# Node scores by GpSimd products and VectorE sums, and denominators summed inside layer 0, in a four-layer graph network kernel

## The chip, the cores and the metric

The kernel runs on one core of a Trainium2 chip. A core has five engines that each work through their own instructions in order and wait for one another through semaphores: TensorE (PE, matrix products into PSUM; its weight loads are listed as PEld), VectorE (DVE), ScalarE (ACT), GpSimd (POOL) and SyncE (SP, which only issues DMAs here). The metric is the device time of one execution in microseconds, lower is better.

## What is computed

The input is x with 8 batches of 2048 nodes of 64 features, and a 2048 x 2048 adjacency matrix. Four graph layers follow, each as `x = layernorm(x + layer(x))`. Layer 0 is a graph convolution with weights mixed for each node from an embedding of 16 numbers; layer 1 is a hypergraph attention; layers 2 and 3 are plain graph convolutions. The change touches the end of layer 0's loop, where the first steps of layer 1 are done already for the rows that are finished:

```python
h = x @ W
s = jax.nn.leaky_relu(h @ a_node, 0.2)
logits = jnp.where(maskEN[None, :, :] > 0, s[:, None, :], NEG)
alpha = jax.nn.softmax(logits, axis=-1)
agg = jnp.einsum('ben,bnf->bef', alpha, h)
beta = jax.nn.sigmoid((h @ a_gn)[:, None, :] + (agg @ a_ge)[:, :, None])
...
industry = jnp.einsum('nm,bmf->bnf', adj / deg, x @ W_ind)
```

So each node needs, for each of the 8 batches, two scores: `h @ a_node`, whose exp becomes its softmax weight, and `h @ a_gn`. The softmax is done without dividing first: `aggp` sums exp(s) h over the nodes of each hyperedge, `denp` sums exp(s), and `agg` is their quotient.

## The kernel before

The nodes are cut into 16 rows of 128 (NT = 16), and a row's tile is 128 nodes x 512 numbers (8 batches x 64 features, B = 8, C = 64). float32 products run as two passes on TensorE, which is why the profile counts 8 for 4 of them.

**Layer 0** (`layer0`) is one loop over j from 0 to 16. Turn j does the 8 weighings of row j (`weigh`, g = 0 to 7): 24 matmuls each (L1035) into one of two PSUM tiles, and four VectorE instructions (L1046) that read this tile and add it to the row's residue r. Between the weighings stand the other steps, some of row j, some of the row behind (j - 1, j - 2) and some of the rows ahead (j + 1, j + 2). All of it stands in `program_order`, which ties the instructions of each engine into exactly the order in which they are written. Nothing can overtake on its engine. In a turn:

- after weighing 0, 1 and 2: the three steps of the norm of row j - 1 (`normed`: sum, centring and square; sum of squares and root; reciprocal and the two products that give x1). After weighing 1 also `scaled` (GpSimd: the mask of the next row times its scale, `ms`, and the count tree `cs`).
- after weighing 2: `first_terms` of row j + 1: GpSimd adds y_hi and y_lo to y1 (L971), TensorE transposes y1 (`try`, in a helper, L152) and multiplies the bias (`bp`, L979), ScalarE copies both, GpSimd makes the new residue r (L984).
- after weighing 3: the whole y2 product of row j + 1 (L998, 32 matmuls), the transposes of x1 of row j - 1 (`to_features`, `trx`), compares and masks on VectorE.
- after weighing 6: `second_term` (four transposes), `scores` of row j - 1, `gather` of row j - 2.
- after weighing 7: `degrees`, and `project` of row j - 1: 8 products (`hp`, L1113) give h and the industry part; ScalarE copies h (L1129), then the high part of the industry (L1130), VectorE forms the low part (L1131), and GpSimd multiplies h by exp(s) to `hs` (L1138).

`scores` works from the transposed x1: `wa` holds W a_node and W a_gn, computed once in `load_weights`, and four products per row (`sgp`, L1092) give both scores. `gather` (L1143) adds `hs` times the hyperedge memberships `md` into `aggp`.

**Layer 1** (`layer1`) starts with `md` for all rows on GpSimd (L551), 16 products for the denominators (`denp`, L556), their reciprocal `rden`, and `agg`.

The last turn (j = 16) has no weighings: it is a plain chain of norm, transposes, scores, gather, h and gather for row 15.

Of the kernel before, what the change touches and what calls it, by code (L numbers as in the profile page):

```python
# [8 lines left out]
F32 = mybir.dt.float32  # L9
# [9 lines left out]
P = 128  # L19
# [27 lines left out]
def r_(ap):  # L47
    return ap.bitcast(F32R)
# [3 lines left out]
def kernel(  # L52
# [454 lines left out]

    @with_exitstack
    def layer1(
        stack, own, wts, fcw_sb, fcb_sb, av_sb, fcg_sb, vecs, pm, es, hgr, aggp, agg_st, h_sb,  # L510
        i_hi, i_lo, mask_tile, times_mask,
    ):

# [20 lines left out]
        with tc.tile_pool(name="fa", bufs=2) as fa:  # L534
# [10 lines left out]
                for n, k in (("ftr", 1), ("fmm", 1))  # L545
            )
            with program_order():
                md = fa.tile([P, NT, 2, E], F32, tag="md", name="md", bufs=1)
                for q in range(NQ):
                    t = slice(4 * q, 4 * q + 4)  # L550
                    nc.gpsimd.tensor_copy(  # L551
                        md[:, t], pm[:, t].unsqueeze(2).to_broadcast([P, 4, 2, E])
                    )
                denp = ps_tr.tile([P, B], F32, tag="den", name="denp")
                for j in range(NT):
                    nc.tensor.matmul(  # L556
                        denp, md[:, j].rearrange("p h e -> p (h e)"), es[:, j, :],
                        start=j == 0, stop=j == NT - 1,
                    )
                rden = fa.tile([P, B], F32, tag="rden", name="rdene", bufs=1)  # L560
                nc.vector.tensor_scalar(rden, denp, TINY, None, op0=ALU.max)
                nc.vector.reciprocal(rden, rden)
                agg = fa.tile([P, BC], F32, tag="hs", name="agg", bufs=3)
                nc.vector.tensor_tensor(b_view(agg), b_view(aggp), bcast(rden), ALU.mult)

# [329 lines left out]
    def layer0(  # L895
# [3 lines left out]

        h_sb, wb, wa, vecs, av_sb, pm, es, hgr, aggp = layer1s
        raws, msk, terms, resid, norm, srow = {}, {}, {}, {}, {}, {}
        x1s, xTs, hps, hss, mds = {}, {}, {}, {}, {}

# [181 lines left out]
            nc.scalar.copy(xTs[j], tr)  # L1087

        def scores(j):
            sp = ps_tr.tile([P, NP, 2, 2], F32, tag="tr", name=f"sgp_{j}")  # L1090
            for pr in range(NP):
                nc.tensor.matmul(  # L1092
                    sp[:, pr].rearrange("p i h -> p (i h)"), xTs[j][:, pr, :],
                    wa.rearrange("p i h -> p (i h)"), start=True, stop=True,
                )
            sg = tile("sg", f"sg_{j}", (P, NP, 2))
            nc.scalar.copy(sg, sp[:, :, 0, :])
            nc.scalar.copy(hgr[:, j, 0, :].rearrange("p (r h) -> p r h", h=2), sp[:, :, 1, :])
            ej = es[:, j, :]
            nc.vector.scalar_tensor_tensor(  # L1100
                ej.rearrange("p (r h) -> p r h", h=2), sg, 0.2, sg, op0=ALU.mult, op1=ALU.max
            )
            nc.vector.tensor_scalar(ej, ej, TOP, None, op0=ALU.min)
            nc.scalar.activation(ej, ej, AF.Exp)

        def project(j):

            mm = ps_p.tile([P, 2, 2, 4 * C], F32, tag="pp", name=f"hp_{j}")
            mm = mm.rearrange("p h l (m x) -> p h (l m) x", m=2)
            for pr in range(NP):  # L1110
                for h in range(2):
                    rs = slice(h * 64, (h + 1) * 64)
                    nc.tensor.matmul(  # L1113
                        mm[:, h, pr, :], xTs[j][rs, pr, :], wb[rs], start=True, stop=True
                    )
            md = tile("md", f"md_{j}", (P, 2, E))
            nc.gpsimd.tensor_copy(md, pm[:, j, :].unsqueeze(1).to_broadcast([P, 2, E]))
            mds[j] = md.rearrange("p h e -> p (h e)")

            def by_half(t):  # L1120
                return t.rearrange("p (r h c) -> p h r c", h=2, c=C)


            stay = j >= len(kept_i)
            if stay:
                hi, lo = y_hi[:, j, :], y_lo[:, j, :]
            else:
                hi, lo = (tile(k, f"{k}_{j}", bufs=1) for k in ("ihi", "ilo"))
            nc.scalar.copy(by_half(h_sb[:, j, :]), mm[:, :, :, 0:C])  # L1129
            nc.scalar.copy(r_(by_half(hi)), mm[:, :, :, C:2 * C])  # L1130
            nc.vector.tensor_tensor(  # L1131
                r_(by_half(lo)), mm[:, :, :, C:2 * C], by_half(hi), ALU.subtract
            )
            if not stay:
                for t, kept_part in zip((hi, lo), kept_i[j]):
                    nc.sync.dma_start(kept_part, t)
            hss[j] = tile("hs", f"hs_{j}", bufs=1)
            nc.gpsimd.tensor_tensor(  # L1138
                b_view(hss[j]), b_view(h_sb[:, j, :]), bcast(es[:, j, :]), ALU.mult
            )  # L1140

        def gather(j):
            nc.tensor.matmul(aggp, mds[j], hss[j], start=j == 0, stop=j == NT - 1)  # L1143

        box = tile("box", "flagbox", (P, 256), 1)
        flags = lists_flag(
            box, lambda: ps_tr.tile([P, QW], F32, tag="tr", name="flagp"), pm, wb[:, 0:C],
# [14 lines left out]
        with program_order():  # L1162
# [6 lines left out]
            for j in range(NT + 1):  # L1169
                first = j == 0  # L1170
                if not first:
                    when(j + 2, load_adj)
                when(j + 2, load_x)
                for g in range(8):
                    when(j, weigh, g)
                    if g == 0:
                        when(j - 1, normed, 0)
                        if first:
                            compare(0, 0)
                            compare(0, 1)  # L1180
                            load_adj(2)
                    elif g == 1:
                        when(j - 1, normed, 1)
                        if first:
                            degrees(0)
                        when(j + 1, scaled, 0)
                    elif g == 2:
                        when(j - 1, normed, 2)
                        when(j + 1, first_terms)
                    elif g == 3:  # L1190
                        if j + 1 < NT:
                            for _ in product(j + 1):
                                pass
                        when(j - 1, to_features)
                        when(j + 1, compare, 0)
                        when(j + 1, scaled, 1)
                        if j == NT - 2:
                            for t in range(len(kept_i)):
                                for y, kept_part in zip((y_hi, y_lo), kept_i[t]):
                                    nc.sync.dma_start(y[:, t, :], kept_part)  # L1200
                        when(j + 2, mask, 0)
                        when(j + 2, mask, 1)
                    elif g == 5:
                        when(j + 1, compare, 1)
                        if j:
                            next(flags, None)
                    elif g == 6:
                        when(j + 1, second_term)
                        when(j - 1, scores)
                        when(j - 2, gather)  # L1210
                    elif g == 7:
                        when(j + 1, degrees)
                        when(j - 1, project)
            gather(NT - 1)


    def short_program(top):
# [7 lines left out]


        wb = wts.tile([P, 2 * C], F32, tag="wb", name="wb")
        wa = wts.tile([P, 2, 2], F32, tag="wa", name="wa")
        vecs = wts.tile([P, 3, C], F32, tag="vecs", name="vecs")
        pm = wts.tile([P, NT, E], F32, tag="pm", name="pm")  # L1230
        es = wts.tile([P, NT, B], F32, tag="es", name="es")
        hgr = wts.tile([P, NT, 2, B], F32, tag="hgr", name="hgr")
        fcg_sb = wts.tile([P, 1], F32, tag="fcg", name="fcg_sb")

        def load_weights():
# [8 lines left out]
            block_diag(w2_sb[:, 1, :], w2n)  # L1244
            nc.sync.dma_start(bias2_sb, bias2.partition_broadcast(P))
            block_diag(w3_sb, w3t)
            nc.gpsimd.memset(wa, 0.0)
            prod = wts.tile([P, C], F32, tag="prod", name="prod")
            for h in range(2):
                s = slice(h * 64, (h + 1) * 64)  # L1250
                for i in range(2):
                    nc.vector.tensor_tensor(prod[s], wb[s, 0:C], vecs[s, i, :], ALU.mult)
                    nc.vector.tensor_reduce(wa[s, i, h:h + 1], prod[s], AX.X, ALU.add)

        def prepare(ps, pre):
            for h in range(2):
# [27 lines left out]
        with tc.tile_pool(name="l0", bufs=1) as l0, tc.tile_pool(  # L1284
# [14 lines left out]
            with tc.tile_pool(name="l0s", bufs=2) as l0s, tc.tile_pool(  # L1299
# [3 lines left out]
            ) as ps_p:  # L1303
                layer0(
                    own, l0s, rawp, mskp, ps_acc, ps_tr, ps_p, w_sb, emb_sb, bias_sb, bad, deg,
                    y_hi, y_lo, (h_sb, wb, wa, vecs, av_sb, pm, es, hgr, aggp),
                )
                s1, dinv = cols_of["s1"], cols_of["dinv"]
                nc.vector.tensor_tensor(deg, deg, s1, ALU.mult)
# [15 lines left out]


        x2 = layer1(
            own, wts, fcw_sb, fcb_sb, av_sb, fcg_sb, vecs, pm, es, hgr, aggp, agg_st, h_sb, y_hi,
            y_lo, mask_tile, times_mask,
        )  # L1330

# [695 lines left out]
```

## Time and profile before

| | us |
|---|---|
| median of 3 runs | 1388.19 (1386.91 to 1389.96) |
| profiled execution | 1406.12, of which its span 1404.0 |
| start to 154 (first product) | 154.0, TensorE busy 142.3 |
| 204.4 to 695.8 (steady rows of layer 0) | 491.4, TensorE busy 479.6, VectorE 375.0, GpSimd 215.7, ScalarE 96.8 |
| one such row, 485.40 to 520.46 | 35.06, TensorE busy 34.27, VectorE 26.53, GpSimd 16.01, ScalarE 6.92 |
| 723.3 to 748.4 (the last turn, up to the first exp of layer 1) | 25.1, TensorE busy 16.5, granted clock 0.57 |

The busy times are of single engines, which overlap. The span is the time between the first and the last instruction on the chip in the profiled execution; the times of the other runs are without the profiler. In the lines of the timeline each line has its start, its length, the engine, the line of the code, the operation, what is written and read, how many instructions were merged, and in square brackets how long the engine had been idle and what ended that.

### The profile page before, as it was taken

How to read it: one execution, taken by the hardware profiler on the slowest of the kernel's cores; microseconds unless marked ns; L12 is line 12 of the kernel's file. 1: busy time of each engine (PE TensorE's matmuls, PEld its weight loads, DVE VectorE, ACT ScalarE, POOL GpSimd, SP SyncE). 2: the span in 40 equal slices, each digit the busy share in tenths (PEclk: the TensorE clock that was granted, in tenths of full speed). 3: DMA queues.
4: the chain of work that ended last, by engine and by line, in shares of the span. 5: the costliest groups of instructions: out<-in, count | busy, mean ns of one | idle time of the engine just before them, and what ended most of it. 6: DMA issues, size and time to landing. Idle time of an engine off the chain costs nothing.

```text
span 1404.0 us, 19827 instructions
## 1 busy us (share of the span) xinstructions
PE 1323.9 (94%) x7692; PEld 1033.8 (74%) x7692; DVE 931.5 (66%) x1658; ACT 364.1 (26%) x844; POOL 444.2 (32%) x373
## 2 busy tenths in 40 slices
PE   8999889999999999999977799999998799999997
PEld 6777678888888888888855466666666588888885
DVE  4555357787777777777753767678885666665554
ACT  3000101111111111111221345456665321111111
POOL 0000444444444444444201454546663420000000
PEclk9999999999999999999985788899999899999999
DMA  9865323333333333331504121222220213333551
GB/s 307 210 185 171 124 92 101 100 101 100 100 100 100 100 100 100 100 99 53 210 23 151 52 75 38 75 76 76 75 76 1 91 60 120 120 120 136 180 187 70
DMA packets 91047, 153.00 MB, mean 109 GB/s; under 512 B 12097, under 2 KB 55489, under 8 KB 84673
## 3 DMA queue, kind: packets, MB, share of 16 engines
q1 hardware_dynamic: 88642, 147.46, 31.6%
q10 hardware_dynamic: 2304, 4.20, 0.8%
q8 instruction: 63, 1.03, 0.3%
q14 instruction: 38, 0.31, 0.1%
HBM read 115.97 MB, written 35.66 MB: 108 GB/s over the span
## 4 chain that ended last, share of the span: by engine, by line
PE 91%; DVE 4%; issue 2%; ACT 1%; POOL 1%; DMA 1%; SPq 0%; ACTq 0%; DVEq 0%; POOLq 0%
PE pp L1035 23%; PE a L1273 17%; PE ind L1273 9%; PE y2p L998 9%; PE y1p L469 9%; PE fc L813 3%; PE u L1356 2%; PE df L822 2%; PE gp L708 2%; PE trm L152 1%; PE dp L733 1%; PE try L152 1%; PE aggp L1143 1%; PE hp L1113 1%; PE yp L1385 1%
## 5 line engine op out<-in xcount | busy, mean ns | idle before, releaser
L1046 DVE SCALAR_TENSOR_TENSOR r<-pp,emb_sb,r 128x256 f32<-128x256 f32 x512 | 247.3, 483 | 132.1 <-PE pp L1035 117.5
L1035 PE MATMUL pp<-w_sb,xT 64*128 64x256 f32 x1024 | 163.1, 391 | 11.9 <-PE hp L1113 10.3
L1035 PE MATMUL pp<-w_sb,y1T 64*128 64x256 f32 x1024 | 156.3, 377 | 0.0
L1035 PE MATMUL pp<-w_sb,y2T 64*128 64x256 f32 x1024 | 156.3, 377 | 0.0
L1035 PEld LDWEIGHTS pp<-w_sb,xT 64*128 64x128 f32 x1024 | 98.1, 188 | 35.1 <-issue 15.5
L749 POOL TENSOR_TENSOR ez<-ez,coef 128x1024 f32<-128x1024 f32 x32 | 65.0, 2032 | 153.9 <-DVE ez L747 131.4
L469 PE MATMUL y1p<-x_hi,m 128*128 128x512 f32 x256 | 107.0, 418 | 7.1 <-ACT x_hi L417 7.0
L1035 PEld LDWEIGHTS pp<-w_sb,y1T 64*128 64x128 f32 x1024 | 103.8, 188 | 7.7
L1035 PEld LDWEIGHTS pp<-w_sb,y2T 64*128 64x128 f32 x1024 | 103.8, 188 | 7.7
L1273 PE MATMUL ind<-y_hi,mj_l 128*128 128x512 f32 x256 | 107.1, 418 | 0.7 <-DVE dlt L778 0.7
L998 PE MATMUL y2p<-y_hi,msk 128*128 128x512 f32 x256 | 103.8, 406 | 0.0
L1273 PE MATMUL a<-y_hi,mj_l 128*128 128x512 f32 x256 | 102.5, 401 | 0.0
L469 PE MATMUL y1p<-x_lo,m 128*128 128x512 f32 x256 | 102.3, 400 | 0.0
L998 PE MATMUL y2p<-y_lo,msk 128*128 128x512 f32 x256 | 102.0, 399 | 0.0
L1273 PE MATMUL a<-y_lo,mj_l 128*128 128x512 f32 x256 | 101.6, 397 | 0.0
L1273 PE MATMUL ind<-y_lo,mj_l 128*128 128x512 f32 x256 | 101.5, 396 | 0.0
L1273 PE MATMUL a<-v_hi,mj_l 128*128 128x512 f32 x256 | 100.5, 393 | 0.0
L1273 PE MATMUL a<-v_lo,mj_l 128*128 128x512 f32 x256 | 100.1, 392 | 0.0
L1138 POOL TENSOR_TENSOR hs<-h,es 128x512 f32<-128x512 f32 x16 | 16.7, 1042 | 237.6 <-DVE r L1046 195.4
L950 POOL TENSOR_TENSOR ms<-msk,srow 128x1024 f32<-128x1024 f32 x32 | 77.4, 2418 | 6.4 <-DVE ms L963 5.7
L1273 PEld LDWEIGHTS ind<-y_hi,mj_l 128*128 128x128 f32 x256 | 49.0, 192 | 34.2 <-issue 17.7
L971 POOL TENSOR_TENSOR y<-y_hi,y_lo 128x512 f32<-128x512 f32 x16 | 25.7, 1609 | 133.5 <-PE y1p L469 133.5
(262 smaller groups left out, 2499.2 us busy)
## 6 DMA issues: line engine op xcount, KB each, us to landing
mj_l<-mask SPq DMA_DIRECT2D x48, 1024.0 KB, 4.9
raw<-in_at SPq DMA_DIRECT2D x32, 512.0 KB, 4.8
adj<-in_at SPq DMA_DIRECT2D x64, 256.0 KB, 3.4
mask<-msk SPq DMA_DIRECT2D x32, 512.0 KB, 3.1
xraw<-in_xn SPq DMA_DIRECT2D x8, 512.0 KB, 5.6
oh<-oh SPq DMA_DIRECT2D x16, 256.0 KB, 3.8
xT<-in_xt SPq DMA_DIRECT2D x16, 256.0 KB, 3.0
xs<-in_xn SPq DMA_DIRECT2D x16, 256.0 KB, 2.7
```

What stands on the lines that cost most here:

```text
L152: nc.tensor.matmul(dst, src, ident, start=True, stop=True, is_transpose=True)
L469: nc.tensor.matmul(accs[q][jj], r_(m[:, t, jj * P:(jj + 1) * P]), r_(part[:, mt, :]), start=i + h + t == 0 and part is x_hi, stop=i == 3 a ...
L708: nc.tensor.matmul(gp[:, u, :], r_((oh01, oh23)[i][rs, cols]), r_(part[rs]), start=part is agg_hi, stop=part is agg_lo,)
L749: nc.gpsimd.tensor_tensor(by_b(ez), by_b(ez), per_b(coef, 2 * i, 2), ALU.mult)
L813: nc.tensor.matmul(fc[:, h, :], fcw_sb[rs], sT[rs], start=True, stop=True)
L822: nc.tensor.matmul(df[:, b:b + 1], th[:, b % 2, (b // 2) * P:(b // 2 + 1) * P], av_sb, start=True, stop=True,)
L950: nc.gpsimd.tensor_tensor(ms, m, srow[j].unsqueeze(1).to_broadcast([P, 8, P]), ALU.mult)
L998: nc.tensor.matmul(acc, r_(msk[j, mt // 8][:, mt % 8, :]), r_(part[:, mt, :]), start=mt == 0 and part is y_hi, stop=mt == NT - 1 and part ...
L1035: nc.tensor.matmul(pp[:, h, pl, :], terms[j][name][rs, 2 * bq + pl], w_sb[rs, k, dq * 4 * C:(dq + 1) * 4 * C], start=k == 0, stop=k == K - 1,)
L1046: nc.vector.scalar_tensor_tensor(rb, ppv[:, :, dd, :], emb_sb[:, j, d:d + 1], rb, op0=ALU.mult, op1=ALU.add)
L1273: nc.tensor.matmul(acc, r_(a[:, mt, :]), r_(part[:, mt, :]), start=mt == 0 and part is hi, stop=mt == NT - 1 and part is lo,)
L1356: nc.tensor.matmul(mm[:, i], xT[:, 2 * p2 + i, :], w2_sb, start=True, stop=True)
```

## The change

- `scores` no longer uses TensorE. After h is copied, `project` lets GpSimd multiply h by a_node (into `hss[j]`) and by a_gn (into the tile of x1, which is no longer needed then). `scores` sums each over the 64 features with VectorE, makes the exp as before, and then GpSimd forms h times exp(s).
- `scores` moves from after weighing 6 of the next turn to after weighing 1 of the turn after it (row j - 2 instead of j - 1, as it now needs h).
- `project` copies the high part of the industry ahead of h.
- The denominators are summed at the start of the last turn for rows 0 to 14 (`spread` writes all memberships again, into free buffers) and for row 15 after its scores. `layer1` gets `rden`. In the last turn `gather` of row 14 moves there too, ahead of the denominators.
- `wa` and its computation go.

On GpSimd this gives the order, in each turn from 2 to 14: h times a_node, h times a_gn, ms, three of cs, h times exp(s), y1. On VectorE: four reads of weighing 1, variance sum, sum of scores, leaky relu, clamp, sum for a_gn, four reads of weighing 2. On ScalarE: root, change of table, exp.

```diff
         def scores(j):
-            sp = ps_tr.tile([P, NP, 2, 2], F32, tag="tr", name=f"sgp_{j}")
-            for pr in range(NP):
-                nc.tensor.matmul(
-                    sp[:, pr].rearrange("p i h -> p (i h)"), xTs[j][:, pr, :],
-                    wa.rearrange("p i h -> p (i h)"), start=True, stop=True,
-                )
-            sg = tile("sg", f"sg_{j}", (P, NP, 2))
-            nc.scalar.copy(sg, sp[:, :, 0, :])
-            nc.scalar.copy(hgr[:, j, 0, :].rearrange("p (r h) -> p r h", h=2), sp[:, :, 1, :])
             ej = es[:, j, :]
-            nc.vector.scalar_tensor_tensor(
-                ej.rearrange("p (r h) -> p r h", h=2), sg, 0.2, sg, op0=ALU.mult, op1=ALU.max
-            )
+            sg = tile("sg", f"sg_{j}", (P, B))
+            nc.vector.tensor_reduce(sg, b_view(hss[j]), AX.X, ALU.add)
+            nc.vector.scalar_tensor_tensor(ej, sg, 0.2, sg, op0=ALU.mult, op1=ALU.max)
             nc.vector.tensor_scalar(ej, ej, TOP, None, op0=ALU.min)
             nc.scalar.activation(ej, ej, AF.Exp)
+            nc.vector.tensor_reduce(hgr[:, j, 0, :], b_view(x1s[j]), AX.X, ALU.add)
+            nc.gpsimd.tensor_tensor(
+                b_view(hss[j]), b_view(h_sb[:, j, :]), bcast(ej), ALU.mult
+            )
...
         def project(j):
...
+            nc.scalar.copy(r_(by_half(hi)), mm[:, :, :, C:2 * C])
             nc.scalar.copy(by_half(h_sb[:, j, :]), mm[:, :, :, 0:C])
-            nc.scalar.copy(r_(by_half(hi)), mm[:, :, :, C:2 * C])
...
             hss[j] = tile("hs", f"hs_{j}", bufs=1)
-            nc.gpsimd.tensor_tensor(
-                b_view(hss[j]), b_view(h_sb[:, j, :]), bcast(es[:, j, :]), ALU.mult
-            )
+            for i, t in enumerate((hss[j], x1s[j])):
+                nc.gpsimd.tensor_tensor(
+                    b_view(t), b_view(h_sb[:, j, :]),
+                    vecs[:, i, :].unsqueeze(1).to_broadcast([P, B, C]), ALU.mult,
+                )
...
+        def spread():
+            mds.clear()
+            for q, home in enumerate((1, 2, 3, 5)):
+                md = own.tile([P, 4, 2, E], F32, tag=f"b0_{home}", name=f"md4_{q}")
+                nc.gpsimd.tensor_copy(
+                    md, pm[:, 4 * q:4 * q + 4].unsqueeze(2).to_broadcast([P, 4, 2, E])
+                )
+                for t in range(4):
+                    mds[4 * q + t] = md[:, t].rearrange("p h e -> p (h e)")
+
+        def denominators(lo, hi):
+            for j in range(lo, hi):
+                nc.tensor.matmul(
+                    denp[0], mds[j], es[:, j, :], start=j == 0, stop=j == NT - 1
+                )
...
                         when(j + 1, scaled, 0)
+                        when(j - 2, scores)
+                        if j == NT:
+                            denp.append(ps_acc.tile([P, BC], F32, tag="acc", name="denp")[:, 0:B])
+                            gather(NT - 2)
+                            spread()
+                            denominators(0, NT - 1)
                     elif g == 2:
                         when(j - 1, normed, 2)
                         when(j + 1, first_terms)
...
                     elif g == 6:
                         when(j + 1, second_term)
-                        when(j - 1, scores)
-                        when(j - 2, gather)
+                        if j < NT:
+                            when(j - 2, gather)
...
+            scores(NT - 1)
+            denominators(NT - 1, NT)
+            nc.vector.tensor_scalar(rden, denp[0], TINY, None, op0=ALU.max)
+            nc.vector.reciprocal(rden, rden)
             gather(NT - 1)
```

More of the change, by code (lines that the diff above doesn't have):

```diff
@@ L509, in layer1 @@
     def layer1(
-        stack, own, wts, fcw_sb, fcb_sb, av_sb, fcg_sb, vecs, pm, es, hgr, aggp, agg_st, h_sb,
+        stack, own, wts, fcw_sb, fcb_sb, av_sb, fcg_sb, vecs, rden, hgr, aggp, agg_st, h_sb,
         i_hi, i_lo, mask_tile, times_mask,
@@ L547, in layer1 @@
             with program_order():
[L548 to L552, printed above, removed]
-                    )
-                denp = ps_tr.tile([P, B], F32, tag="den", name="denp")
-                for j in range(NT):
-                    nc.tensor.matmul(
-                        denp, md[:, j].rearrange("p h e -> p (h e)"), es[:, j, :],
-                        start=j == 0, stop=j == NT - 1,
-                    )
-                rden = fa.tile([P, B], F32, tag="rden", name="rdene", bufs=1)
-                nc.vector.tensor_scalar(rden, denp, TINY, None, op0=ALU.max)
-                nc.vector.reciprocal(rden, rden)
                 agg = fa.tile([P, BC], F32, tag="hs", name="agg", bufs=3)
@@ L898, in layer0 @@
     ):
-        h_sb, wb, wa, vecs, av_sb, pm, es, hgr, aggp = layer1s
+        h_sb, wb, vecs, av_sb, pm, es, hgr, aggp, rden = layer1s
         raws, msk, terms, resid, norm, srow = {}, {}, {}, {}, {}, {}
@@ L1089, in scores @@
         def scores(j):
-            sp = ps_tr.tile([P, NP, 2, 2], F32, tag="tr", name=f"sgp_{j}")
-            for pr in range(NP):
-                nc.tensor.matmul(
-                    sp[:, pr].rearrange("p i h -> p (i h)"), xTs[j][:, pr, :],
-                    wa.rearrange("p i h -> p (i h)"), start=True, stop=True,
-                )
-            sg = tile("sg", f"sg_{j}", (P, NP, 2))
-            nc.scalar.copy(sg, sp[:, :, 0, :])
-            nc.scalar.copy(hgr[:, j, 0, :].rearrange("p (r h) -> p r h", h=2), sp[:, :, 1, :])
             ej = es[:, j, :]
-            nc.vector.scalar_tensor_tensor(
-                ej.rearrange("p (r h) -> p r h", h=2), sg, 0.2, sg, op0=ALU.mult, op1=ALU.max
-            )
+            sg = tile("sg", f"sg_{j}", (P, B))
+            nc.vector.tensor_reduce(sg, b_view(hss[j]), AX.X, ALU.add)
+            nc.vector.scalar_tensor_tensor(ej, sg, 0.2, sg, op0=ALU.mult, op1=ALU.max)
             nc.vector.tensor_scalar(ej, ej, TOP, None, op0=ALU.min)
             nc.scalar.activation(ej, ej, AF.Exp)
+            nc.vector.tensor_reduce(hgr[:, j, 0, :], b_view(x1s[j]), AX.X, ALU.add)
+            nc.gpsimd.tensor_tensor(
+                b_view(hss[j]), b_view(h_sb[:, j, :]), bcast(ej), ALU.mult
+            )
         def project(j):
@@ L1115, in project @@
                     )
-            md = tile("md", f"md_{j}", (P, 2, E))
-            nc.gpsimd.tensor_copy(md, pm[:, j, :].unsqueeze(1).to_broadcast([P, 2, E]))
-            mds[j] = md.rearrange("p h e -> p (h e)")
+            if j < NT - 1:
+                md = tile("md", f"md_{j}", (P, 2, E))
+                nc.gpsimd.tensor_copy(md, pm[:, j, :].unsqueeze(1).to_broadcast([P, 2, E]))
+                mds[j] = md.rearrange("p h e -> p (h e)")
             def by_half(t):
@@ L1137, in project @@
             hss[j] = tile("hs", f"hs_{j}", bufs=1)
-            nc.gpsimd.tensor_tensor(
-                b_view(hss[j]), b_view(h_sb[:, j, :]), bcast(es[:, j, :]), ALU.mult
-            )
+            for i, t in enumerate((hss[j], x1s[j])):
[3 more added lines that the diff above has]
+                )
         def gather(j):
             nc.tensor.matmul(aggp, mds[j], hss[j], start=j == 0, stop=j == NT - 1)
+        def spread():
[12 more added lines that the diff above has]
+                )
+        denp = []
         box = tile("box", "flagbox", (P, 256), 1)
@@ L1227, in short_program @@
         wb = wts.tile([P, 2 * C], F32, tag="wb", name="wb")
-        wa = wts.tile([P, 2, 2], F32, tag="wa", name="wa")
         vecs = wts.tile([P, 3, C], F32, tag="vecs", name="vecs")
@@ L1231, in short_program @@
         es = wts.tile([P, NT, B], F32, tag="es", name="es")
+        rden = wts.tile([P, B], F32, tag="rden", name="rden")
         hgr = wts.tile([P, NT, 2, B], F32, tag="hgr", name="hgr")
@@ L1246, in load_weights @@
             block_diag(w3_sb, w3t)
[L1247 to L1253, printed above, removed]
         def prepare(ps, pre):
@@ L1305, in short_program @@
                     own, l0s, rawp, mskp, ps_acc, ps_tr, ps_p, w_sb, emb_sb, bias_sb, bad, deg,
-                    y_hi, y_lo, (h_sb, wb, wa, vecs, av_sb, pm, es, hgr, aggp),
+                    y_hi, y_lo, (h_sb, wb, vecs, av_sb, pm, es, hgr, aggp, rden),
                 )
@@ L1327, in short_program @@
         x2 = layer1(
-            own, wts, fcw_sb, fcb_sb, av_sb, fcg_sb, vecs, pm, es, hgr, aggp, agg_st, h_sb, y_hi,
+            own, wts, fcw_sb, fcb_sb, av_sb, fcg_sb, vecs, rden, hgr, aggp, agg_st, h_sb, y_hi,
             y_lo, mask_tile, times_mask,
```

## The prediction

> **What bounds the kernel now.** I first read the busy line and the clock row of the page, then the chain of waits over one row of layer 0, then the timeline of the same stretch engine by engine, because the change touches layer 0 and the step right after it only.
>
> ```profile
> PE 1323.9 (94%) x7692; PEld 1033.8 (74%) x7692; DVE 931.5 (66%) x1658; ACT 364.1 (26%) x844; POOL 444.2 (32%) x373
> ```
>
> TensorE is busy nearly always. In the chain of waits (start, length, what) one row runs from 485.40 to 520.46, and nearly all of it is TensorE:
>
> ```profile
> 485.40 8.04 PE pp L1035 x72
> 493.44 0.58 PE try L152 x4
> 494.03 0.36 PE bp L979 x2
> 494.39 2.79 PE pp L1035 x24
> 497.18 7.55 PE y2p L998 x32
> 504.73 0.44 PE trx L152 x4
> 505.16 7.97 PE pp L1035 x72
> 513.13 0.59 PE try L152 x4
> 513.72 0.79 PE sgp L1092 x8
> 514.51 0.96 PE aggp L1143 x2
> ...
> 519.70 0.76 issue
> ```
>
> A row is 35.06 us. The three first weighings are 8.04, then TensorE transposes y1 of the next row (`try`, in `first_terms`). The scores (`sgp`) take 0.79. Where does y1 come from? The timeline of GpSimd, VectorE and ScalarE at the start of the next row (start 520.46):
>
> ```profile
> 520.38 1.04 POOL L1138 TENSOR_TENSOR hs<-h,es 128x512 f32<-128x512 f32 x1 [14.26 <-DVE r L1046]
> 521.38 2.35 POOL L950 TENSOR_TENSOR ms<-msk,srow 128x1024 f32<-128x1024 f32 x1
> ...
> 526.26 1.72 POOL L971 TENSOR_TENSOR y<-y_hi,y_lo 128x512 f32<-128x512 f32 x1
> ...
> 526.77 2.03 DVE L1046 SCALAR_TENSOR_TENSOR r<-pp,emb_sb,r 128x256 f32<-128x256 f32 x4
> ...
> 528.72 0.68 DVE L1063 TENSOR_REDUCE var_l<-sq_l 128x8 f32<-128x512 f32 x1
> ...
> 529.43 0.30 ACT L1065 ACTIVATE std_l<-var_l,eps_t 128x8 f32<-128x8 f32 x1 [0.54 <-DVE var_l L1063]
> ```
>
> y1 ends at 527.98; TensorE wants it at 520.46 + 8.04 = 528.50. The spare time is half a microsecond, and GpSimd works without a gap from 520.38 to there. What happens when y1 is late stands in row 0, where GpSimd began late:
>
> ```profile
> 179.11 1.11 PE L152 MATMUL try<-ident,y 128*128 128x128 f32 x4 [4.78 <-POOL y L971]
> 180.15 0.69 PE L979 MATMUL bp<-bias_sb,et 16*128 16x64 f32 x2
> 180.77 1.23 PE L1035 MATMUL pp<-w_sb,xT 64*128 64x256 f32 x4
> ```
>
> TensorE waited 4.78 us and then ran slow: four transposes 1.11 against 0.66 elsewhere, and the 24 products behind them 4.32 in the chain (180.84 to 185.16) against 2.79.
>
> **What the Trainium skill says.** "TensorE: Matmul & The Clock Gate", part 1 (The HAM clock gate): an idle window of about 3.4 us halves the clock, and about as much sustained work restores it, in windows that run freely. Row 0 agrees: a wait of 4.78 us, then slow work for some 4.5 us. "ScalarE: Activation LUTs", What ACT_TABLE_LOAD costs: 1283 ns and a drain of 1380 for a change of table. The trace has the 1283 (16 loads before the exp, mean 1283), but no such drain: at 725.46 the load follows the square at once, and the root follows the load at 726.76. I use 1.28. "SBUF — State Buffer", Who interferes with whom: GpSimd and VectorE exclude each other at one port pair when VectorE reads two SBUF tensors or is in a two-port mode, while a reduction never does. L954 took 2.28 beside the masks of L942 and 1.27 beside L1046, which fits.
>
> **The change, part by part.**
> *Removed from TensorE:* `sgp`, 0.79 in a steady row, where nothing replaces it on TensorE. The end of the row (weighing 7, 2.19 until the next row starts, set by VectorE's four reads of weighing 7) stays. So -0.8 in rows 1 to 15.
> *Added to GpSimd:* after `h`, two products (h by a_node, h by a_gn), where there was one; then, at step 1 of the next row, the product by es. In the order of GpSimd's instructions, this last one stands behind ms and cs and ahead of y1. It waits for the exp, and y1 waits behind it, and TensorE's in-order queue behind y1 (try, bp, weighing 3, the whole y2 product). A product of this kind is 1.04 (L1138), at most 1.27 (L593, he by a_ge, the same broadcast).
> *When is the exp done?* With the row of 520.46: VectorE cannot reach the new sums before its variance sum; that one frees it at 529.31 (where the next L1046 starts now). Sum of the scores 0.71 (start to dependent start, as from L1054 at 525.32 to L1055 at 526.03) to 530.02; leaky relu and clamp 0.2 each to 530.4. ScalarE's root ends at 529.73, the change to the exp table takes until 531.03, so the table is last, and the exp (0.21) ends at 531.24. GpSimd: product 531.3 to 532.3, y1 1.72 to 534.0, TensorE starts at 534.1 instead of 528.5. The stall is 5.6 us, 11 times the spare time.
> *Without any wait for es,* the queue alone: two more products (2.1) and h copied 0.5 later (the swap at ScalarE) put y1 at 530.6, a stall of 2.1; that is the floor.
> *Clock after the stall:* row 0 lost 0.46 + 0.26 + 1.53 = 2.25 after a shorter wait. From nothing (no idle window hit) to 2.8 (the first y2 product at 154.10: 10.32 against 7.55). I take 2.0.
> *VectorE* gets two sums of 0.68 a row and has 26.5 busy of 35.06; with the row longer it is no bound. Weighing 2 is read 1.8 later, but weighing 3 comes 5.6 later still. The masks, compares and degrees of the next row keep their place relative to TensorE. h's copy after the industry part, md and the DMAs issued by SP (same number and order) cost nothing on the path: they lie beside 8.04 of weighing; GpSimd has 16.0 busy of 35.
> *Rows with both halves of it* (scores of j-2 and y1 of j+1): j = 2 to 14, 13 rows. Each: 5.6 - 0.8 + 2.0 = +6.8, so +88.4. Row 1: -0.8. Row 15 has no y1, but TensorE already waits there for VectorE's normed x (0.56 at 707.17): four new VectorE instructions push it by 1.8, less 0.98 of sgp: +0.9.
> *The end of layer 0,* counted from the last row's first sum (723.30), now 25.06 to the first exp of layer 1 (748.36). New: variance sum to 726.15, scores of row 14 to 727.3 on VectorE, root, table and exp to 728.6 on ScalarE, GpSimd 729.7, gather 1.91 to 731.65, 30 denominator matmuls at 7.01/32 = 0.22 to 738.2, and only then the transposes of x (ready at 728.8): trx 1.11, copy 0.6, hp 2.0, to 742.1. Industry 0.6 and h 0.5, two products 2.1, sum, clamp and exp beside the second, product by es to 746.8, gather 2.1 to 748.9, agg 0.7, exp at 749.65. So +1.3: the denominators are off the tail (7.01 and md 0.7), but TensorE does them while x waits, and a longer way through h, product, sum, exp, product replaces sgp. Bounds -3 to +3.
> *First stage:* eight small VectorE instructions and one GpSimd memset go, beside TensorE's work: 0.
>
> Sum: 88.4 - 0.8 + 0.9 + 1.3 = +89.8. Against the profiled execution (1406.1, span 1404.0) that is 1496; the median of the runs is 1388.2, 18 lower, and the difference carries over: 1478.
>
> **Rivals.**
> (a) Only GpSimd's queue counts: the exp is early enough, so the stall is 2.1, too short to lose the clock. 13 x (2.1 - 0.8) + 1.4 = +18, 1406. For it: GpSimd's own chain is a fact; against it: the sums stand behind the variance on VectorE.
> (b) The ports: the product by es and y1 (2.8) now run beside the normed x (L1072, two SBUF inputs), and stretch as L954 did, by 1.0 to 2.7 a row: +103 to +125, 1491 to 1513. Against it: L1072 is only 0.76 long.
> (c) Faster: TensorE doesn't stand still for y1, so that only the -0.8 of 15 rows and the tail count: -12 + 1 = -11, 1377. The mechanism is that GpSimd reaches y1 in time: it must start by 526.7 (528.5 less 1.8). That would be so if y1 came ahead of the product by es in GpSimd's order and the two products after h fitted into gaps. Against it: the built order has the product by es first, and there are no gaps between 520.38 and 527.98, so even with y1 first the extra product and the later h would leave y1 some 1.0 late. The gain of 0.8 a row is outweighed from a stall of 0.8 on.
> (d) The clock never drops, stall as forecast: 13 x 4.8 + 1.4 = +64, 1452.
>
> **How the numbers follow.** Forecast with its own clock losses 0.70 (1458 to 1496), (d) 0.10, (b) 0.10, (a) 0.07, (c) 0.03. The range reaches from (d) at 1450 to a stall of 6.4 with 2.6 of clock loss, 13 x 8.2 + 3 = +110, 1498, and takes in the lower half of (b). About 0.2% (2.8 us) is what a measurement of this kernel can tell from no change. Faster is (c), 0.03; same 0.01, a stall of 0.8 by chance; slower the rest, 0.96.
>
> **What would show it.** In the changed trace: transposes of y1 with a wait of over 5 us for GpSimd in 13 rows, each with 1.1 instead of 0.66 behind it in most; the product by es starting just after an exp, which starts at the end of a table load; rows of about 42 instead of 35; TensorE's busy share down to about 90%; no `denp` after the last gather. It is wrong if the table load is elsewhere, if y1 precedes the product by es, or if the wait for y1 is under 2 us.

## The result, and where the time went

The changed kernel takes 1495.76 us (1494.57 to 1497.67, 4 runs) against 1389.08 for the kernel before: 1.0771 times as long, 95% interval 1.0753 to 1.079. That is 106.7 us more; the prediction had 90, 1478, and a range from 1450 to 1500.

The profiled execution that the prediction worked from (1406.1) turned out not to be typical. I therefore profiled the kernel before once more (`before_again`, 1388.88), and the stages are compared with that one. The table by stages (stretch, its length, busy time of each engine with its instructions, granted clock, share and rate of the DMAs) is cut at the start of row 1, the start of row 15, the last row's first sum and the first exp of layer 1. The granted clock is the share of full speed that the trace records for TensorE. First the kernel before, then the changed one:

```profile
204.00:694.67 490.67, 478.81 (x3720) 405.21 (x3717) 374.51 (x690) 96.67 (x195) 215.72 (x190) 1.00 0.32 105
694.67:722.20 27.53, 25.55 (x222) 21.30 (x222) 20.93 (x49) 5.89 (x13) 2.33 (x4) 1.00 0.07 21
722.20:747.26 25.06, 16.50 (x66) 12.56 (x66) 6.43 (x18) 5.60 (x10) 3.54 (x6) 0.52 0.42 119
747.26:1386.80 639.54, 598.69 (x2808) 440.19 (x2808) 427.96 (x658) 229.92 (x582) 186.89 (x130) 0.95 0.27 93
```

```profile
203.90:797.52 593.62, 506.50 (x3614) 419.31 (x3613) 362.66 (x716) 93.78 (x165) 232.74 (x216) 0.90 0.26 87
797.52:825.72 28.20, 24.38 (x214) 21.01 (x214) 21.61 (x50) 5.64 (x11) 4.37 (x5) 1.00 0.07 20
825.72:853.49 27.77, 14.18 (x58) 11.10 (x58) 9.80 (x24) 5.57 (x10) 8.76 (x10) 0.52 0.28 95
853.49:1493.80 640.31, 600.95 (x2808) 441.73 (x2808) 427.69 (x658) 229.87 (x582) 186.08 (x130) 0.94 0.26 94
```

The rows 1 to 14 carry it: +102.95. Row 15 is 0.67 longer, the last turn 2.71, and all later work is the same within 0.8. In the rows TensorE has 106 fewer instructions and yet 27.7 us more busy time, and its granted clock fell from 1.00 to 0.90. Its idle time in the rows went from 11.9 to 87.1. So the time has two parts: TensorE waits, and it is slower. The page's line of busy times shows the first of the two, 89% for TensorE where it was 94%:

```profile
PE 1333.1 (89%) x7564; PEld 1037.6 (69%) x7564; DVE 922.6 (62%) x1682; ACT 360.3 (24%) x810; POOL 467.1 (31%) x403
```

One row of the changed kernel, in the chain of waits (start, length, what):

```profile
495.44 2.88 PE pp L1020 x24
...
501.01 1.52 DVE r L1040
...
504.48 0.59 DVE var_l L1048
505.07 0.60 DVE sg L1078
...
506.07 0.59 DVE hgr L1082
506.66 0.40 DVE r L1031
...
508.05 1.23 POOL y L956
509.28 0.04 issue
509.33 1.12 PE try L152 x4
510.44 0.61 PE bp L964 x2
511.06 5.26 PE pp L1020 x24
516.32 7.54 PE y2p L983 x32
```

Before, only TensorE stood in this chain. Now the first weighing leads into VectorE's centring (L1040), variance sum and sum of scores (L1078), then to y1 on GpSimd (L956), and back to the transposes of y1. Chain pieces between 506 and 508 are VectorE's next work; who really held y1 is seen on ScalarE and GpSimd, in the timeline of the same row:

```profile
505.11 0.30 ACT L1050 ACTIVATE std_l<-var_l,eps_t 128x8 f32<-128x8 f32 x1 [0.53 <-DVE var_l L1048]
505.43 1.28 ACT L1081 ACT_TABLE_LOAD   x1
506.72 0.21 ACT L1081 ACTIVATE es<-es 128x8 f32<-128x8 f32 x1
```

```profile
495.89 1.29 POOL L1122 TENSOR_TENSOR hs<-h,vecs 128x512 f32<-128x512 f32 x1 [17.72 <-ACT h L1112]
497.13 1.30 POOL L1122 TENSOR_TENSOR x<-h,vecs 128x512 f32<-128x512 f32 x1
...
507.01 1.04 POOL L1083 TENSOR_TENSOR hs<-h,es 128x512 f32<-128x512 f32 x1 [3.36 <-ACT es L1081]
508.01 1.26 POOL L956 TENSOR_TENSOR y<-y_hi,y_lo 128x512 f32<-128x512 f32 x1
```

GpSimd had done everything else by 503.6, stood still 3.36 us for the exp, and only then got to y1. What it does to TensorE, in TensorE's timeline:

```profile
509.33 1.12 PE L152 MATMUL try<-ident,y 128*128 128x128 f32 x4 [5.85 <-POOL y L956]
510.37 0.69 PE L964 MATMUL bp<-bias_sb,et 16*128 16x64 f32 x2
510.99 1.23 PE L1020 MATMUL pp<-w_sb,xT 64*128 64x256 f32 x4
```

A wait of 5.85, and work at about half speed behind it: four transposes take 1.12 instead of 0.66, and the weighing after them 5.26 in the chain instead of 2.79. The trace records a granted clock of 0.50 from 505.80 to 516.00. So it goes in all of rows 2 to 14: the waits for y1 are 5.19 to 5.85, 5.74 on average, and a row takes 43.04 on average instead of 35.16.

### The profile page after: what moved, and what is told of

It is laid out like the page before. It is cut to its first block, busy times and chain, and to the rows that moved or that the text cites. A ratio compares the mean times of both kernels' runs of the same rounds, so it can differ in the third digit from the quotient of the medians.

```text
span 1493.8 us, 19605 instructions
## 1 busy us (share of the span) xinstructions
PE 1333.1 (89%) x7564; PEld 1037.6 (69%) x7564; DVE 922.6 (62%) x1682; ACT 360.3 (24%) x810; POOL 467.1 (31%) x403
## 4 chain that ended last, share of the span: by engine, by line
PE 81%; DVE 11%; issue 3%; POOL 2%; ACT 1%; DMA 1%; SPq 0%; ACTq 0%; POOLq 0%; DVEq 0%
PE pp L1020 19%; PE a L1279 16%; PE ind L1279 9%; PE y2p L983 8%; PE y1p L469 8%; DVE r L1031 5%; PE fc L798 2%; PE u L1362 2%; PE df L807 2%; PE try L152 2%; PE gp L693 2%; DVE r L1040 1%; PE trm L152 1%; POOL y L956 1%; PE yp L1391 1%
## 5 line engine op out<-in xcount | busy, mean ns | idle before, releaser
L1020 PE MATMUL pp<-w_sb,xT 64*128 64x256 f32 x1024 | 174.7, 416 | 12.6 <-PE hp L1094 9.5
L1020 PE MATMUL pp<-w_sb,y1T 64*128 64x256 f32 x1024 | 166.5, 399 | 0.0
L1020 PE MATMUL pp<-w_sb,y2T 64*128 64x256 f32 x1024 | 165.9, 398 | 0.0
L1020 PEld LDWEIGHTS pp<-w_sb,xT 64*128 64x128 f32 x1024 | 104.4, 200 | 37.9 <-PE hp L1094 11.5
L1020 PEld LDWEIGHTS pp<-w_sb,y1T 64*128 64x128 f32 x1024 | 110.5, 201 | 10.7
L1020 PEld LDWEIGHTS pp<-w_sb,y2T 64*128 64x128 f32 x1024 | 110.2, 200 | 10.6
L1122 POOL TENSOR_TENSOR hs<-h,vecs 128x512 f32<-128x512 f32 x16 | 20.6, 1286 | 301.0 <-ACT h L1112 301.0
L152 PE MATMUL try<-ident,y 128*128 128x128 f32 x128 | 27.6, 353 | 82.5 <-POOL y L956 79.5
L152 PEld LDWEIGHTS try<-ident,y 128*128 128x128 f32 x128 | 17.6, 174 | 94.2 <-POOL y L956 85.1
```

Of the source, the lines that this page charges most:

```text
L152: nc.tensor.matmul(dst, src, ident, start=True, stop=True, is_transpose=True)
L1020: nc.tensor.matmul(pp[:, h, pl, :], terms[j][name][rs, 2 * bq + pl], w_sb[rs, k, dq * 4 * C:(dq + 1) * 4 * C], start=k == 0, stop=k == K - 1,)
```

## The experiments

The theory: y1 waits in GpSimd's queue behind a product that waits for the exp, TensorE waits for y1, and in the wait it loses its clock. The rivals: the longer queue of GpSimd alone makes the stall; ports shared by VectorE and GpSimd stretch everything; what is slow after the wait is not the clock. Line numbers below are those of each experiment's own code.

**y1 ahead of the product.** `first_terms` gives its sum of y_hi and y_lo to a function of its own, `first_sum`:

```diff
                         when(j + 1, scaled, 0)
+                        when(j + 1, first_sum)
                         when(j - 2, scores)
```

> The changed kernel, with y1 of the next row added on GpSimd before the product by exp(s) instead of behind it. Theory (y1 waits behind a product that waits for the exp): the 3.4 us that GpSimd stands still goes, y1 ends about 505.3 in a row that starts at 495.44, TensorE waits about 1.9 us instead of 5.85, too short for the clock to fall, four transposes of y1 take 0.66 again; a row is about 36.2, total about 1407. Rival (the longer GpSimd queue alone makes the stall): no real change, above 1480. Rival (ports shared by VectorE and GpSimd stretch everything): about 1440 to 1470, with stretched sums and products.

Measured: 1408.46 (1.0107 times before, 1.0048 to 1.0166). In its timeline, GpSimd and then TensorE:

```profile
498.57 1.27 POOL L957 TENSOR_TENSOR y<-y_hi,y_lo 128x512 f32<-128x512 f32 x1
501.97 1.04 POOL L1088 TENSOR_TENSOR hs<-h,es 128x512 f32<-128x512 f32 x1 [2.14 <-ACT es L1086]
```

```profile
499.89 0.66 PE L152 MATMUL try<-ident,y 128*128 128x128 f32 x4 [1.44 <-POOL y L957]
```

The product still waits for the exp, but nothing that TensorE needs is behind it. Of the stall of 5.85 there are 1.44 left, which the two products after h and the later copy of h make, and the four transposes take 0.66 again. Moving one instruction of 1.3 us past another gave back 87 of the 107 us.

The queue that is left is worth 1.44 - 0.8 = 0.6 a row in most rows. In 4 of the 11 rows with a wait of about 1.44, though, the weighing behind it was slow, as here behind the wait that ended at 282.22:

```profile
283.24 4.48 PE pp L1025 x24
```

The granted clock is 0.50 from 283.80 to 287.20. So these four rows lost another 1.7 each; I had expected a wait this short to leave the clock alone.

**y1 a turn earlier,** so that the queue's 1.44 goes too:

```diff
                     elif g == 7:
+                        when(j + 2, first_sum)
                         when(j + 1, degrees)
```

> The changed kernel, with y1 of the row after next added on GpSimd at the end of the turn, ahead of md and the two products. Theory: TensorE no longer waits for y1 at all, 15 rows lose the 0.8 of the scores' products against the kernel before, the tail stays about 3 us longer: 1389 - 12 + 3 = 1380. Rival (something else is late once y1 is in time, for example VectorE with its two sums or x1 for its transposes): rows stay above 35.1 and the time is at or above 1389.

Measured: 1386.77 (0.9969 times before, 0.9955 to 0.9983). TensorE no longer waits for y1; rows are 34.43 instead of 35.06. I expected 34.27 and 1380. In its chain of waits, weighing 3 is now released by VectorE's read of weighing 1:

```profile
486.97 1.51 DVE r L1045
488.48 0.41 DVE r L1036
...
489.95 0.49 DVE r L1036
490.45 0.14 issue
490.58 2.86 PE pp L1025 x24
```

Weighing 3 needs the PSUM tile that weighing 1 filled. The centring (L1045) took 1.51 where it took 0.8 before, and that makes VectorE late by about 0.2 a row. So the scores' move saves 0.6 in a steady row, 7.4 us over rows 1 to 14, once y1 is out of the way; the end of layer 0 takes part of that back.

**The product with an old exp,** to take away the wait for the exp and leave the order:

```diff
-                b_view(hss[j]), b_view(h_sb[:, j, :]), bcast(ej), ALU.mult
+                b_view(hss[j]), b_view(h_sb[:, j, :]),
+                bcast(es[:, max(j - 1, 0), :]), ALU.mult
```

> The changed kernel, but the product on GpSimd takes the exp of the row before instead of its own, so that h is weighted by the wrong row's numbers and aggp is not the reference's; the exp itself is still made. Order and number of instructions are unchanged, only the wait for the fresh exp is gone. Theory: y1 follows the queue of GpSimd without a gap and ends at about 506, TensorE waits 2.5 to 3 us instead of 5.85, and loses the clock in few rows or none: 1405 to 1425. Rival (the queue alone): as the changed kernel, above 1480.

Measured: 1471.87 in one run. A miss. GpSimd, VectorE and TensorE in its timeline:

```profile
496.13 1.04 POOL L1083 TENSOR_TENSOR hs<-h,es 128x512 f32<-128x512 f32 x1 [2.10 <-DVE sg L1078]
497.13 1.26 POOL L956 TENSOR_TENSOR y<-y_hi,y_lo 128x512 f32<-128x512 f32 x1
```

```profile
495.38 0.68 DVE L1078 TENSOR_REDUCE sg<-hs 128x8 f32<-128x512 f32 x1
```

```profile
498.45 1.12 PE L152 MATMUL try<-ident,y 128*128 128x128 f32 x4 [4.57 <-POOL y L956]
```

I had overlooked that the product writes over the very tile that VectorE is summing. Without the exp it still waits 2.10 for the end of that sum. So the exp, with its table load, was the last 1.3 us of two waits one behind the other; the larger share, 2.1, is the wait for the sum, which stands on VectorE behind the variance of another row. A stall of 4.57 still costs the clock: the transposes took 1.12 in 12 of the 13 rows, and the weighing behind them 4.31 on average (4.96 in the changed kernel). That is why only 24 us came back.

**The wait filled.** Is it the clock? 24 products of no use stand ahead of the transposes of y1, and keep TensorE busy in the wait. In the first attempt:

```diff
             tr = ps_tr.tile([P, NP, P], F32, tag="tr", name=f"try1_{j}")
+            if j > 2:
+                for _ in range(24):
+                    nc.tensor.matmul(
+                        tr[:, 0:2].rearrange("p r c -> p (r c)"), terms[j]["x"][0:64, 0],
+                        w_sb[0:64, 0, 0:4 * C], start=True, stop=True,
+                    )
```

> The changed kernel, with 24 products (48 passes, about 5.4 us at full clock) into the transposes' own PSUM tile ahead of the transposes of y1, in rows 3 to 15; their result is overwritten. TensorE's wait is filled but y1 is as late as before. Theory (each row loses about 3.0 us because the clock falls in the wait): transposes of y1 take 0.66, weighing 3 takes 2.8, rows of about 40.1 instead of 43.15, total about 1496 - 12 x 3.0 = 1459. Rival (what is slow behind the wait is not the clock but the operands or PSUM): rows stay at 43 or get longer, 1496 or more.

Measured: 1515.45 in one run. The filling took 10.5 us instead of 5.4, longer than the wait, so the total says nothing on the clock. The weighing behind it does: it took 2.79 in all 13 rows, and the granted clock over rows 2 to 14 is 1.00 (0.90 in the changed kernel). These products all used one half of the array's rows and wrote to one place in PSUM, where the weighings alternate between the halves and between two places. The second attempt does so too:

```diff
+            if j > 2:
+                fill = ps_tr.tile([P, QW], F32, tag="tr", name=f"fill_{j}")
+                for n in range(24):
+                    rs = slice(64 * (n % 2), 64 * (n % 2) + 64)
+                    nc.tensor.matmul(
+                        (tr[:, 0:2].rearrange("p r c -> p (r c)"), fill[:, 0:256])[n % 2],
+                        terms[j]["x"][rs, 0],
+                        w_sb[rs, 0, 0:4 * C], start=True, stop=True,
+                    )
```

> As stall_filled, but the 24 products alternate between the two halves of the rows and two PSUM tiles, as the weighings do, so that the 48 passes should take the 5.4 us of two weighings and end before y1 is there. Results of the filling are overwritten or never read. Theory (clock): y1 is as late as in the changed kernel, TensorE's remaining wait is under 1 us, weighing 3 takes 2.8 instead of 4.2 to 5.4; rows of 40.1 instead of 43.15, total about 1496 - 12 x 3.0 = 1460. Rival (not the clock): about 1496.

Measured: 1458.47 in one run. TensorE in its timeline:

```profile
533.63 0.38 PE L962 MATMUL fill<-w_sb,xT 64*128 64x256 f32 x1
534.61 0.66 PE L152 MATMUL try<-ident,y 128*128 128x128 f32 x4 [0.61 <-POOL y L956]
535.20 0.43 PE L973 MATMUL bp<-bias_sb,et 16*128 16x64 f32 x2
535.56 0.70 PE L1029 MATMUL pp<-w_sb,xT 64*128 64x256 f32 x4
```

This row starts at 520.78; y1 is as late as in the changed kernel (transposes 13.83 after the row's start, 13.89 there), but they take 0.66 and the weighing behind them 2.79, in this row and in the 12 others. Rows 2 to 14 are 40.32 on average instead of 43.04, and their granted clock is 0.99. The extra work made the kernel 37.3 us faster. That is 2.9 for each of 13 rows. As the operands are the same, it settles that the half speed comes from TensorE's idling and not from them.

**The parts alone, on the kernel before.** First, the industry's high part ahead of h, with the two copies in `project` exchanged and nothing else:

> The kernel before with the part on the industry alone: its high part copied ahead of h. h, and with it GpSimd's product, ms, cs and y1 come 0.5 us later, the low part on VectorE 0.4 to 0.5 earlier, where VectorE waits for the next weighing anyway. Theory (0.5 us of spare time of y1 covers it exactly): y1 ends within 0.1 us of the time TensorE wants it, 0 to 0.1 a row, 1389 to 1391. Rival (the swap opens a wait of its own at y1): up to 0.5 a row, 1397. Rival (the earlier low part helps): below 1386.

Measured: 1388.98 (0.998 times before, 0.9962 to 0.9998), rows of 35.06. The half microsecond of spare time at y1 covers it; at most some tenths of a per cent lie in it.

Second, the denominators: `spread` and `denominators` as in the changed kernel, with scores by TensorE:

> The kernel before with the denominators' part alone: summed in the last turn as in the changed kernel, scores still by TensorE. Theory (the part is good, but spoilt in the changed kernel by the scores that come late): gather and denominators fall into TensorE's wait for the norm, transposes of x some 4 us later, denominators (7.0) and md (0.7) gone behind the last gather: last turn about 19 instead of 25, total about 1383. Rival (the delay of the transposes eats what the tail gains): 1387 to 1391.

Measured: 1383.12 (0.9942 times before, 0.992 to 0.9964). From the last row's first sum to the first exp of layer 1 it takes 15.59 instead of 25.06:

```profile
722.15 4.38 PE L1144 MATMUL denp<-es,md 128*128 128x8 f32 x30
...
726.38 1.09 PE L152 MATMUL trx<-ident,x 128*128 128x128 f32 x4
```

Row 14's scores are done in time there, so the denominators fall into TensorE's wait for the norm. That is more than I expected, also because TensorE keeps its clock for some of them (4.38 for 30, against 7.0 for 32 before). Of these 9.5 us the span shows 5.9: the work after the first exp of layer 1 took 644.17 instead of 639.54 in this trace, at a granted clock of 0.93 instead of 0.95. What causes that is open.

**The end of layer 0.** In the changed kernel the same 30 products stand in the way. From its timeline:

```profile
833.26 2.08 PE L1128 MATMUL aggp<-hs,md 128*128 128x512 f32 x2 [9.30 <-POOL hs L1083]
...
835.13 6.41 PE L1143 MATMUL denp<-es,md 128*128 128x8 f32 x30
...
841.39 1.09 PE L152 MATMUL trx<-ident,x 128*128 128x128 f32 x4
```

x is ready at 832.16, but its transposes are at 841.39: the gather of row 14 waits for GpSimd (that row's own exp), and denominators and transposes stand behind it. So, on top of `y1_turn_earlier`, the gather and the denominators go behind `project` of the last row:

```diff
-                            gather(NT - 2)
                             spread()
-                            denominators(0, NT - 1)
...
+            gather(NT - 2)
+            denominators(0, NT - 1)
             scores(NT - 1)
             denominators(NT - 1, NT)
```

> y1_turn_earlier with the end of layer 0 reordered: in the last turn TensorE first transposes x and makes h, and does the gather of row 14 and the denominators after that, while ScalarE, GpSimd and VectorE work on h. Theory (TensorE's 6.4 us of denominators and 2 of the gather hold up the transposes of x): from the last row's first sum to the first exp of layer 1 about 22 instead of 27.8, total about 1381. Rival (the chain through GpSimd's two products, the sum, the exp and the product ends last anyway): no more than 1 us gained, 1386.

Measured: 1376.93 (0.9898 times before, 0.9879 to 0.9916), 1% faster than the kernel before; 19.16 from the first sum to the exp. From its timeline:

```profile
724.02 1.11 PE L152 MATMUL trx<-ident,x 128*128 128x128 f32 x4 [7.92 <-DVE x L1062]
...
729.68 3.98 PE L1148 MATMUL denp<-es,md 128*128 128x8 f32 x32
```

The transposes now start as soon as x is there, and the denominators lie beside GpSimd's and VectorE's work on h.

**The kernel before once more,** unchanged:

> The kernel before, unchanged, for a second trace. The first profiled execution was 17 us above the median of the runs, and between the first exp of layer 1 and the end it took 655.6 against 640.3 in the changed kernel, which does the same work there. Expected if that was a hiccup of one execution: 640 there, rows of 35.05 and a last turn of 25 as in the first trace, total 1388 to 1391. Rival (the change also makes layer 1 some 15 us faster): 655 there again and a total of about 1405.

Measured: 1388.88, one run; 639.54 from the first exp of layer 1 to the end, 35.05 us rows and a last turn of 25.06. The 17 us of the first trace were of that execution, which took 655.64 for the same work at a granted clock of 0.92 instead of 0.95, and the change doesn't touch layer 1.

## Why the prediction was right, and where it was off

The mechanism was the one forecast, step by step; the price of the slow work behind the wait was too low, and the result lies near the upper edge of the range.

- *Spare time of half a microsecond, and y1 behind the product.* Right. The exp came just after the table load (505.43 + 1.28, exp at 506.72), the product just after the exp, y1 after it. Forecast stall 5.6, measured 5.85 in the row shown and 5.74 on average. Two terms were off and partly cancelled: VectorE's centring took 1.52 instead of 0.8, and y1 itself 1.26 instead of 1.72. The products by a_node and a_gn took 1.29, at the upper bound. The 5.85 is made of the queue after h (1.44 by `y1_before_product`), the product by es (1.04) and GpSimd's wait for the exp (3.36). So the queue alone, with that product, is an estimated 2.5 where the prediction had 2.1.
- *Minus 0.8 for the scores.* Right within the reach of these runs: y1_turn_earlier has it as 0.6, less the 0.2 of VectorE's delay.
- *The clock after the stall: this is the term that was too small.* I took 2.0 a row, from a bracket of nothing to 2.8, below row 0's 2.25, on the thought that some waits would miss an idle window. None did. In all 13 rows the weighing after the wait was slow (4.17 to 5.42, mean 4.96, against 2.79), the transposes lost 0.54 and the bias product 0.25, and sometimes the y2 product began slow too: about 3.05 a row from the chain of waits, 2.9 by the filled wait. The 2.25 was a single sample. In the second trace of the same kernel the same wait in row 0 (4.77) is followed by a weighing of 5.33 instead of 4.32, and in the changed kernel (4.78) by one of 5.42. Nor does the loss depend on the stall alone: behind the waits of 4.57 in `product_old_exp` it was about 2.3 a row. The term accounts for 13 x 1.05 = 13.7 of the 17 us that the sum missed, the stall for 13 x 0.14 = 1.8, and the last turn for 1.4.
- *Row 15:* +0.9 forecast (its terms, 1.8 less 0.98, give 0.8), +0.67 measured. *Last turn:* +1.3 forecast, +2.7 measured, within its bounds. The order of its events was as forecast (gather of row 14, 30 denominators, transposes of x, h, product, sum, exp, product, gather). The centring again took longer (1.78 instead of 0.69), and the products 1.3 instead of 1.04.
- *Carrying the 18 us between the profiled execution and the median over* as a constant: the first trace's surplus lay behind layer 0. It did no harm to the difference, as only layer 0 was used. That the sum before this step, 1496, equals the measured time is chance: the surplus of the first trace happens to be as large as what the sum missed.

Of the rivals, (a), the queue alone, is a true effect but not the whole. That `y1_before_product` came to 1408, near its 1406, is luck in part: there the product by es is out of the queue, the wait is 1.44 instead of 2.1, and four rows lose clock, which (a) had ruled out. (b), ports: GpSimd's product and y1 did not stretch (1.04 and 1.26). What got longer is VectorE's work, the centring (1.52 instead of 0.8) and the normed x beside y1 (1.13 at 508.75, instead of 0.76); that the ports are the cause is not shown. (d), no loss of clock, is refuted. (c), faster, is reached in its direction by `y1_turn_earlier` (1386.77, where (c) had 1377), with the condition that I gave for it (GpSimd reaches y1 in time) and not with the change as it is.

## What to carry to other kernels

Where engines work in a fixed order, ask for each instruction that gains a wait what stands behind it in its queue and who needs that. Here a product of 1 us with no hurry held back a sum of 1.3 us on which TensorE's whole row hung, and moving that sum gave back 87 of 107 us. Price a wait of TensorE with the slow work behind it: here 2.3 us a row at waits of 4.57 and 3 at waits of 5.74, about half as much again as the wait itself. One sample of it is not a price, as the same wait in row 0 shows. Work moved into a gap of an engine pays only if its inputs are there when the gap begins: the same denominators saved time when row 14's exp was ready, and delayed the transposes when it was not.

## What the runs showed of the hardware that was not expected

TensorE lost its clock in every one of 13 rows at waits of 5.19 to 5.85 us, in every one of 13 rows at waits of 4.03 to 5.02 (`product_old_exp`), and in 4 of 11 rows at waits of about 1.44 (`y1_before_product`). What sets these four apart from the other seven no run shows. Behind the waits of the changed kernel TensorE stayed slow for 4.4 to 7.9 us of work. In the trace's record of the clock its stretches at 0.50, which begin within the wait, are 6.8 us long in 5 of these rows and 10.2 in 8; in 12 of the 13 rows of `product_old_exp` they are 6.8.

The centring on VectorE, which reads two SBUF tensors, takes 0.69 when GpSimd is idle (row 15 in the kernel before), 1.52 when a GpSimd sum of the counts starts just before it (500.69 against 501.01), and 1.78 when a product of GpSimd does in the last turn (826.41 against 826.43). In return y1 took 1.72 in the kernel before, where it started during a centring, and 1.26 to 1.27 in the changed kernel and in its variants, where it didn't. This fits what the Trainium skill says in "SBUF — State Buffer", Who interferes with whom: a VectorE instruction with two SBUF inputs and a GpSimd instruction that reads SBUF exclude each other, and the later one waits. No run here was made to separate it from other causes.

The same 48 passes of a 64-row product took 5.4 us when they alternated between the two halves of the array's rows and between two places in PSUM, and 10.5 us on one half and one place. Which of the two makes the difference was not separated.
